# Mixture of experts: where the sorted units' way back onto the tokens stands, and which unit comes last

## The chip, the cores and the metric

The kernel runs on one core of a Trainium2 chip. The metric is the device time of one execution in microseconds (us), taken as the median of several runs. Engines are named as in the profile: PE (TensorE, matrix products), PEld (its loads of the stationary operand), DVE (VectorE), ACT (ScalarE), POOL (GpSimd) and SP (SyncE, which here only issues DMA transfers; its queue is SPq).

## The reference

One sequence of 128 tokens with 512 channels goes through three layers: attention over 12,544 context rows, self-attention with block-scaled weights, and a mixture of 32 experts. The change is in the last one, which adds this to the tokens:

```python
def _gate(x, gate_w, gate_bias):            # 4 of 32 experts for each token, weights that sum to 2
    ...
def _moe(x, topk_idx, topk_w, w1, w2, w3):  # H = 512 channels, F = 256 inside an expert
    ...
    h = silu(einsum('ech,ehf->ecf', buf, w1)) * einsum('ech,ehf->ecf', buf, w3)
    ob = einsum('ecf,efh->ech', h, w2)
    y = ob[flat_e, minimum(slot, CAP - 1)]
    ...
    return (y.reshape(n, K, H) * topk_w[:, :, None]).sum(1)
out = _moe(x, topk_idx, topk_w, w1, w2, w3)
shared = silu(x @ shared_gate) * (x @ shared_up) @ shared_down
x = x + out + shared
```

Each expert has 1.5 MB of weights in float32: w1 and w3 (512 x 256 each) and w2 (256 x 512).

## The kernel before

`fast_block` does the three layers; the mixture is its last stage, from about 950 us on. Everything is in float32, and instructions keep the order in which the program writes them (`pin`).

**Experts and units.** The first 6 experts (`FIXED`) are loaded before the gate is known. The other 26 are sorted on the chip by how many tokens chose them. Then they are worked on in *units*. A unit of kind "all" is one of the six fixed experts, over all 128 tokens. "top" is one of the two experts with most tokens, also over all 128. "wide" holds two experts with up to 64 tokens each, "narrow" four with up to 32 each; for these (`some`) the tokens of each expert were picked into columns of `picked`, and their results are put back onto the tokens by a product with `back`. The letters of L1989 give the order of the 15 units: f for all, n for narrow, t for top, w for wide.

**One unit** has these steps:

- `unit_up` (L2109): the products with w1 and w3, in four chunks of 128 channels, into one bank `up` of 512 columns. An all or top unit has one product of 128 x 512 a chunk; a wide or narrow one has two or four beside each other, in strips of 64 or 32 columns of the array ("128\*64", "128\*32" in the profile).
- `unit_act` (L2128): sigmoid on ACT, two products on DVE, into `moe_hg`. All and top units are multiplied by the gate here.
- `unit_turn` (L2141): two transpositions on PE (`hgt`), copied by ACT into `moe_ht`.
- `unit_down` (L2147): the products with w2. All and top units add them straight to `acc`, the sum over all experts that stays in one PSUM bank; wide and narrow ones write a bank `y`, which ACT copies to one of two `outs` (`moe_att_img`, `moe_qT_txt`).
- `unit_combine` (L2169), for wide and narrow units alone: a product of 128 x 512 of `back` with `outs`, added to `acc`. `back` holds the gates.

Between these stand the shared expert's parts and a test that the fast form is valid (`check_sums`, `flag`).

**The order.** In the loop from L2424, turn u takes unit u through its transposition and its way down, and unit u+1 through its way up, so that ACT and DVE work beside PE. In turn u the way back of unit u-1 stands behind the way up of u+1. The last unit's way up is written out in `last_unit` (L2174): in two halves of 256 columns, so that the sigmoid can start before the second is done, with the way back of unit u-2 in the middle.

**The loads.** Each sorted expert comes in three pieces of 512 KB: k=0 and k=1 for the two halves of its way up, k=2 for its way down. The list of all 78 pieces (L1992) follows the units, and in a unit runs over k first and over its experts then. `release` (L2200) puts a piece's buffer on the list of free ones when the program has written the product that reads it last; `load_more` (L2207) gives the next pieces in the list the next free buffers. All are issued by SP, in order; up to eight are on their way at once. A load waits until the last reader of its buffer is done.

Of the kernel before, what the change touches and what calls it, by code (L numbers as in the profile page):

```python
# [10 lines left out]
AF = mybir.ActivationFunctionType  # L11
ALU = mybir.AluOpType
# [3 lines left out]
P = 128  # L16
D = 512
NC = D // P
# [14 lines left out]
F = 256  # L33
# [737 lines left out]
def fast_block(ctx: ExitStack, tc: tile.TileContext, a: dict, out: bass.AP, amiss: bass.AP):  # L771
    nc = tc.nc
# [65 lines left out]
    def pin(ins):  # L838

        return tc.keep_in_program_order(ins)  # L840
# [46 lines left out]
    def row(tag, name, shape=(P, D)):  # L887
        return xc.tile(list(shape), FP, tag=tag, name=name)
# [7 lines left out]
    with ExitStack() as xs:  # L896
# [24 lines left out]
        m = -(-IMG // 3)  # L921
        blocks.append(("img", 0, IMG, [(o, min(m, IMG - o)) for o in range(0, IMG, m)]))
        for l0 in range(IMG, n_ctx, CHUNK):
            n = min(CHUNK, n_ctx - l0)
# [374 lines left out]
        h = rowp.tile([P, D], FP, tag="h", name="h_x")  # L1299
# [102 lines left out]
        m = heights[1]  # L1402
# [132 lines left out]
        for t in range(tile0[2], tile0[LAST]):  # L1535
            b, part, o, m = tiles[t]
# [4 lines left out]
            if t == SWITCH + 3:  # L1541
                pin(nc.tensor.matmul(
                    avp["txt"].rearrange("p g q -> p (g q)"),
                    lhsT=ident,
                    rhs=kept["av"],
                    start=False,
                    stop=False,
                    skip_group_check=True,
# [47 lines left out]
            elif t == SWITCH + 2:  # L1596
                lp = bank("l_old")
                for i in range(4):
                    r = slice(i * XHD, (i + 1) * XHD)
                    pin(nc.tensor.matmul(  # L1600
                        lp[r, :], lhsT=ones[:, :XHD], rhs=ls_old[i // 2][:, i % 2, :],
                        start=True, stop=True, skip_group_check=True,
# [42 lines left out]
        k, p = pend  # L1645
# [52 lines left out]
    def spare(name, shape=(P, 512)):  # L1698
        return ps_t.tile(list(shape), FP, tag="t", name=name)
# [170 lines left out]
    def w13_of(key, c):  # L1870
        return experts[key, c // 2][:, c % 2 * 512 : c % 2 * 512 + 512]
# [59 lines left out]
    for q in range(4):  # L1931
        for k in range(4):
# [3 lines left out]
                lhsT=aoT[:, j, :],  # L1936
                rhs=wo[q][k // 2][:, k % 2 * D : k % 2 * D + D],
                start=(j == 0),
                stop=(j == SH - 1),
# [6 lines left out]
    def halves(t):  # L1946
        return [x.rearrange("p j f -> p (j f)") for x in (t[:, :8], t[:, 8:])]
# [16 lines left out]
    picked = halves(aoT) + wo[3]  # L1964
# [21 lines left out]
    units = []  # L1986
    wide, narrow, every = some[:n_wide], some[n_wide:], [("all", [(e, 0, P)], None) for e in range(FIXED)]

    for k in "ffffnffntnwwntn":  # L1989
        units.append({"f": every, "n": narrow, "t": top, "w": wide}[k].pop(0))  # L1990
    assert not (every or narrow or top or wide)
    loads = []  # L1992
# [56 lines left out]
    def choose():  # L2049
# [43 lines left out]
    held = {  # L2093
        nm: row(tag, f"moe_{nm}", (P, 2, F))
        for nm, tag in (("sig", "part_kFalse"), ("hg", "part_vFalse"), ("ht", "part_kTrue"))
    }
# [5 lines left out]
    def add_to_acc(lhsT, rhs, last=False):  # L2102
        nonlocal n_acc
        pin(nc.tensor.matmul(acc, lhsT=lhsT, rhs=rhs, start=(n_acc == 0), stop=last))  # L2104
        n_acc += 1
# [3 lines left out]
    def unit_up(u, chunks=range(NC)):  # L2109
        kind, lanes, at_ = units[u]  # L2110
        if chunks[0] == 0:
            ups[u] = spare(f"up_{u}", (P, 2 * F))
        up = ups[u]
        for c in chunks:
            for i, r, m in lanes:
                lhsT = hT3[:, c, :] if kind != "some" else picked[c][:, at_ * P + r : at_ * P + r + m]
                pin(nc.tensor.matmul(  # L2117
                    up[r : r + m, :],
                    lhsT=lhsT,
                    rhs=w13_of((kind != "all", i), c),  # L2120
                    start=(c == 0),
                    stop=(c == NC - 1),
                    skip_group_check=True,
                ))
        if chunks[-1] == NC - 1:
            release(u, range(2))

    def unit_act(u):  # L2128
        kind, lanes, at_ = units[u]
        up = ups.pop(u)  # L2130
        sig = held["sig"][:, u % 2, :]
        hg = held["hg"][:, u % 2, :]
        pin(nc.scalar.activation(sig, up[:, :F], AF.Sigmoid))
        if kind == "some":
            pin(nc.vector.tensor_tensor(hg, up[:, :F], sig, ALU.mult))
        else:
            by = (gate if kind == "all" else gate_of)[:, lanes[0][0] : lanes[0][0] + 1]
            pin(nc.vector.scalar_tensor_tensor(hg, up[:, :F], by, sig, ALU.mult, ALU.mult))
        pin(nc.vector.tensor_tensor(hg, hg, up[:, F:], ALU.mult))

    def unit_turn(u):  # L2141
        tp = bank(f"hgt_{u}", (P, 2, P))
        for k in range(2):
            pin(nc.tensor.transpose(tp[:, k, :], held["hg"][:, u % 2, k * P : (k + 1) * P], ident))
        pin(nc.scalar.copy(held["ht"][:, u % 2, :].rearrange("p (k q) -> p k q", k=2), tp))
# [23 lines left out]
    def unit_combine(u):  # L2169
        if units[u][0] == "some":  # L2170
            k = units[u][2]
            add_to_acc(back[:, k * P : (k + 1) * P], outs[u % 2], u == len(units) - 1)

    def last_unit():  # L2174

        u = len(units) - 1
        _, lanes, at_ = units[u]
        up = [spare(f"up_{u}_{h}", (P, F)) for h in range(2)]
        for h, c in [(0, 0), (1, 0), (0, 1), (1, 1), (0, 2), (0, 3), (1, 2), (1, 3)]:
            if (h, c) == (0, 2):  # L2180
                unit_combine(u - 2)
            for i, r, m in lanes:
                pin(nc.tensor.matmul(
                    up[h][r : r + m, :],
                    lhsT=picked[c][:, at_ * P + r : at_ * P + r + m],
                    rhs=w13_of((True, i), c)[:, h * F : (h + 1) * F],
                    start=(c == 0),
                    stop=(c == NC - 1),
                    skip_group_check=True,
                ))  # L2190
            if (h, c) == (0, 3):
                sig = held["sig"][:, u % 2, :]
                pin(nc.scalar.activation(sig, up[0], AF.Sigmoid))
                hg = held["hg"][:, u % 2, :]
                pin(nc.vector.tensor_tensor(hg, up[0], sig, ALU.mult))
        pin(nc.vector.tensor_tensor(hg, hg, up[1], ALU.mult))

    index_of = {}

# [149 lines left out]
    def shared_up(nm):  # L2349
        sp[nm] = bank(nm)  # L2350
        for c in range(NC):
            pin(nc.tensor.matmul(
                sp[nm], lhsT=hT3[:, c, :], rhs=shared[nm][c], start=(c == 0), stop=(c == NC - 1)
            ))
        if nm == "shared_gate":
            pin(nc.scalar.activation(ssig, sp[nm], AF.Sigmoid))
        vec("tensor_tensor", ssig, ssig, sp[nm], ALU.mult)
        free.extend(shared_parts[nm])
        load_more()

    def shared_turn():
        t = bank("tp_shared", (P, NC, P))
        for c in range(NC):
            pin(nc.tensor.transpose(t[:, c, :], ssig[:, c * P : (c + 1) * P], ident))
        pin(nc.scalar.copy(sT, t))

    def shared_down():
        for c in range(NC):
            add_to_acc(sT[:, c, :], shared["shared_down"][c])
        free.extend(shared_parts["shared_down"])  # L2370
        load_more()

    def check_sums():

        top_over = row("top_over", "top_over", (P, 2))
        vec("tensor_reduce", top_over[:, 0:1], over, AX.X, ALU.max)
        vec("tensor_scalar", top_over[:, 0:1], top_over[:, 0:1], FAR, None, ALU.is_gt)
        vec("tensor_scalar", top_over[:, 1:2], n_within, D - 0.5, None, ALU.is_lt)
        far = row("far", "far", (P, 1))
        vec("tensor_tensor", far, top_over[:, 0:1], top_over[:, 1:2], ALU.add)  # L2380

        crowd = row("crowd", "crowd", (P, N_IN + 1))
        vec("tensor_scalar", crowd[:, :N_64], nth[:, :N_64], 64.5, None, ALU.is_gt)
        vec("tensor_scalar", crowd[:, N_64:N_IN], nth[:, N_64:], 32.5, None, ALU.is_gt)
        vec("tensor_reduce", crowd[:, N_IN:], crowd[:, :N_IN], AX.X, ALU.add)
        vec("tensor_tensor", far, far, crowd[:, N_IN:], ALU.add)
        return far

    def flag(far):
        n_far = bank("n_far")  # L2390
        pin(nc.tensor.matmul(n_far[0:1, 0:1], lhsT=far, rhs=ones[:, 0:1], start=True, stop=True))
        vec("tensor_scalar", amiss, n_far[0:1, 0:1], 1.0, None, ALU.min)
# [30 lines left out]
    n = len(units)  # L2423
    for u in range(3, n):  # L2424
        unit_turn(u)
        if u == 5:
            shared_up("shared_gate")
        elif u == 6:
            shared_up("shared_up")
            far = check_sums()  # L2430
        elif u == 7:
            shared_turn()
        elif u == 9:
            flag(far)
        elif u == 11:
            shared_down()
        if u + 1 < n - 1:
            unit_up(u + 1)
            unit_act(u + 1)
        elif u + 1 < n:  # L2440
            last_unit()
        if u != n - 2:
            unit_combine(u - 1)
        unit_down(u)

    unit_combine(n - 1)
    res = rowp.tile([P, D], FP, tag="h", name="res")
    pin(nc.vector.tensor_tensor(res, acc, x2, ALU.add))
    pin(nc.sync.dma_start(out=out, in_=res))
# [80 lines left out]
```

## Time and profile before

| | us |
|---|---|
| median of three runs | 1071.18 (1070.46 to 1071.69) |
| time of the profiled execution | 1070.2 |
| its span | 1068.5 |
| first load of a sorted expert issued | 955.55 |
| last one issued | 1048.46 |
| last product on PE starts | 1061.14 |
| last sum on DVE starts (`res`) | 1062.31 |
| output's transfer issued | 1063.03 |

The span is what the profiler recorded on the core; 1.7 us of the execution's time lie around it. Times inside are from the span's start. PE was busy 1051.4 us of the span, DVE 541.1, ACT 355.8, POOL 694.8; a busy share of PE says little here, since products in flight count as busy while the next waits. The mixture's own stretches, by the windows of the trace, have this PE time and DMA rate:

| stretch, us | PE busy | DMA, GB/s |
|---|---|---|
| 960 to 970 | 10.00 | 396 |
| 1000 to 1010 | 10.00 | 417 |
| 1040 to 1050 | 10.00 | 417 |
| 1050 to 1060 | 9.48 | 282 |
| 1060 to 1068.5 | 1.51 | 40 |

### The profile page before, as it was taken

Reading aid. Unit: us, or ns where it says so; the run is one execution under the profiler, and the core shown is the slowest. Engines: PE = TensorE matmul, PEld = TensorE weight load, DVE = VectorE, ACT = ScalarE, POOL = GpSimd, SP = SyncE. Lnnn points to the kernel's source line nnn. Section 1 sums busy time; section 2 is a strip of 40 time slices with the busy share of each in tenths; the row PEclk is TensorE's granted clock in tenths of the full one; section 3 lists DMA queues with packets and bytes.
Section 4 is the critical chain, followed back from the end, with each engine's and each line's share of the span. In section 5 each row is a group of like instructions: output and inputs, shape, how many; then the busy total and the mean of one; then the engine's idle time right before and its main releaser. Section 6 shows DMA issues by size and latency. Waiting matters only on the chain.

```text
span 1068.5 us, 24782 instructions
## 1 busy us (share of the span) xinstructions
PE 1051.4 (98%) x11076; PEld 826.6 (77%) x11076; DVE 541.1 (51%) x671; ACT 355.8 (33%) x438; POOL 694.8 (65%) x378
## 2 busy tenths in 40 slices
PE   9999999999999999999999999999999989999997
PEld 6778888888888888888888888888888769754332
DVE  3667854574445544455444554455444668432211
ACT  2353333333333333332333333333333424403111
POOL 2256888688988888888988789988899810000000
PEclk9999999999999999999999999999999999999999
DMA  8221021101111011110122301110110399619996
GB/s 318 86 81 41 2 87 44 41 1 41 40 41 40 2 40 41 40 36 7 41 84 106 99 26 41 41 40 3 39 41 2 123 361 382 229 64 410 415 413 247
DMA packets 43251, 113.24 MB, mean 106 GB/s; under 512 B 6720, under 2 KB 12032, under 8 KB 42112
## 3 DMA queue, kind: packets, MB, share of 16 engines
q1 hardware_dynamic: 43136, 111.57, 28.4%
q8 instruction: 89, 1.46, 0.5%
q14 instruction: 26, 0.21, 0.1%
HBM read 111.26 MB, written 0.29 MB: 104 GB/s over the span
## 4 chain that ended last, share of the span: by engine, by line
PE 92%; DVE 3%; POOL 2%; ACT 1%; DMA 1%; issue 0%; SPq 0%; DVEq 0%; ACTq 0%; POOLq 0%
PE kp L1082 28%; PE vp L1082 26%; PE sb L1166 9%; PE av_new L1272 8%; PE up L2117 5%; PE acc L2104 2%; PE qp L1776 1%; PE kp L1776 1%; PE yp L1934 1%; PE svp L1797 1%; PE y L2158 1%; PE vp L1234 1%; PE av_old L1272 1%; DVE p L1255 1%; DMA x<-in_x 1%; POOL sq L1127 1%
## 5 line engine op out<-in xcount | busy, mean ns | idle before, releaser
L1433 POOL TENSOR_TENSOR ls<-ls,p 128x2048 f32<-128x2048 f32 x79 | 359.7, 4553 | 21.3 <-ACT p L1263 21.3
L1263 ACT ACTIVATE p<-p 128x2048 f32<-128x2048 f32 (+1 forms) x95 | 179.9, 1894 | 444.5 <-DVE p L1255 432.9
L1255 DVE SCALAR_TENSOR_TENSOR p<-sb,rinv,mb_new 128x2048 f32<-128x2048 f32 (+1 forms) x86 | 200.0, 2326 | 129.4 <-POOL rinv L818 95.2
L1127 POOL TENSOR_TENSOR sq<-sq 128x512 f32<-128x512 f32 x96 | 96.0, 1000 | 98.2 <-ACT sq L1121 94.4
L1166 PEld LDWEIGHTS sb<-qT_txt,kraw 32*128 32x128 f32 (+1 forms) x3040 | 93.4, 186 | 32.0 <-issue 31.0
L1166 PE MATMUL sb<-qT_txt,kraw 32*128 32x128 f32 (+1 forms) x3040 | 111.5, 283 | 0.0
L1082 PE MATMUL kp<-xs,w_k_w 128*128 128x256 f32 x384 | 95.4, 391 | 0.0
L1082 PE MATMUL kp<-ctx,w_k_w 128*128 128x256 f32 x384 | 93.2, 386 | 1.0 <-ACT kp L1139 1.0
L1272 PE MATMUL av_new<-p,v 128*32 128x128 f32 (+1 forms) x2720 | 92.2, 276 | 1.0 <-ACT p L1263 1.0
L1082 PE MATMUL vp<-vt,xs 128*128 128x256 f32 x384 | 92.5, 384 | 0.0
L1082 PE MATMUL kp<-xs,kt 128*128 128x256 f32 x384 | 91.2, 380 | 0.1
L1082 PE MATMUL vp<-w_v_w,ctx 128*128 128x256 f32 x384 | 90.9, 380 | 0.0
L1082 PE MATMUL vp<-w_v_w,xs 128*128 128x256 f32 x384 | 90.8, 379 | 0.0
L1082 PEld LDWEIGHTS kp<-ctx,w_k_w 128*128 128x128 f32 x384 | 70.7, 190 | 15.0 <-issue 5.1
L1082 PEld LDWEIGHTS vp<-vt,xs 128*128 128x128 f32 x384 | 71.1, 190 | 13.3 <-ACT kraw L1110 4.5
L1082 PEld LDWEIGHTS kp<-xs,kt 128*128 128x128 f32 x384 | 72.5, 190 | 11.3 <-issue 1.1
L1082 PEld LDWEIGHTS vp<-w_v_w,xs 128*128 128x128 f32 x384 | 72.8, 190 | 10.1
L1082 PEld LDWEIGHTS vp<-w_v_w,ctx 128*128 128x128 f32 x384 | 72.8, 190 | 10.0 <-issue 0.2
L1272 PEld LDWEIGHTS av_new<-p,v 128*32 128x32 f32 (+1 forms) x2720 | 69.5, 109 | 12.3 <-ACT p L1263 2.1
L1082 PEld LDWEIGHTS kp<-xs,w_k_w 128*128 128x128 f32 x384 | 69.2, 189 | 12.6 <-issue 4.8
L818 POOL TENSOR_TENSOR rs_x<-ve_x,neghalf 128x1 f32<-128x1 f32 x3 | 1.7, 551 | 94.5 <-DVE ve_x L826 94.5
L1121 ACT ACTIVATE sq<-kraw 128x1024 f32<-128x1024 f32 x48 | 50.0, 1041 | 10.3 <-DVE kraw L1112 10.3
(460 smaller groups left out, 1442.3 us busy)
## 6 DMA issues: line engine op xcount, KB each, us to landing
ctx<-in_ctxT SPq DMA_DIRECT2D x23, 1024.0 KB, 4.9
wo<-in_experts SPq DMA_DIRECT2D x18, 512.0 KB, 9.0
wo<-in_wo_codes SPq DMA_DIRECT2D x8, 512.0 KB, 6.3
wq<-in_experts SPq DMA_DIRECT2D x8, 512.0 KB, 9.8
wk<-in_experts SPq DMA_DIRECT2D x8, 512.0 KB, 9.4
wv<-in_experts SPq DMA_DIRECT2D x7, 512.0 KB, 10.0
q<-in_experts SPq DMA_DIRECT2D x7, 512.0 KB, 10.1
f<-in_experts SPq DMA_DIRECT2D x7, 512.0 KB, 10.1
```

The source lines that it names most:

```text
L1082: pin(nc.tensor.matmul(t[:, h, :], lhsT=lhs, rhs=rhs, start=(first and h == 0 and c == 0), stop=(h == 1 and c == 1), skip_group_check=True,))
L1121: pin(nc.scalar.activation(sq[b][:, :, ks], kraw[b][:, :, ks], AF.Square))
L1127: pin(nc.gpsimd.tensor_tensor(sq[b][:, :w, ks], sq[b][:, :w, ks], sq[b][:, w : 2 * w, ks], op=ALU.add))
L1166: pin(nc.tensor.matmul(s[:m, i, g * P : (g + 1) * P], lhsT=kraw[b][rows, g, o : o + m], rhs=qT[part][rows, g, :], start=True, stop=True,))
L1234: pin(nc.tensor.matmul(vp[:m, :], lhsT=ctx_sb[0][:, c, o : o + m], rhs=vw["img"][:, c, :], start=(c == 0), stop=(c == NC - 1),))
L1255: pin(nc.vector.scalar_tensor_tensor(p[:m, k : k + n], s[:m, k : k + n], rinv[:m, t : t + 1], m_bc[part][:m, k : k + n], ALU.mult, ALU.sub ...
L1263: pin(nc.scalar.activation(p[:m, k : k + n], p[:m, k : k + n], AF.Exp))
L1272: pin(nc.tensor.matmul(avp[part][i * XHD : (i + 1) * XHD, g, :], lhsT=vv[b][:m, t - tile0[b], hd * XHD : (hd + 1) * XHD], rhs=p[:m, i, g * ...
L1433: pin(nc.gpsimd.tensor_tensor(d, d, src, op=ALU.add))
L1776: pin(nc.tensor.matmul(pp[:, k, :], lhsT=w[:, c, k * SHD : (k + 1) * SHD], rhs=hT2[:, c, :], start=(c == 0), stop=(c == NC - 1),))
L2104: pin(nc.tensor.matmul(acc, lhsT=lhsT, rhs=rhs, start=(n_acc == 0), stop=last))
L2117: pin(nc.tensor.matmul(up[r : r + m, :], lhsT=lhsT, rhs=w13_of((kind != "all", i), c), start=(c == 0), stop=(c == NC - 1), skip_group_chec ...
```

## The change

The last two units change places: the order ends with two narrow units and then the second top unit. The way back of unit u-2, no longer that of u-1, stands in turn u, and ahead of the way up of unit u+1 instead of behind it; so a unit's way up is followed at once by the way down of the unit before. In the last turn the way back of unit u-1 follows, ahead of the last way down, which goes straight to `acc`. The last unit's way up is an ordinary `unit_up`, and `last_unit` is gone.

```diff
-    for k in "ffffnffntnwwntn":
+    for k in "ffffnffntnwwnnt":
         units.append({"f": every, "n": narrow, "t": top, "w": wide}[k].pop(0))
...
-    def last_unit():
...
-        for h, c in [(0, 0), (1, 0), (0, 1), (1, 1), (0, 2), (0, 3), (1, 2), (1, 3)]:
-            if (h, c) == (0, 2):
-                unit_combine(u - 2)
...
-        if u + 1 < n - 1:
+
+        unit_combine(u - 2)
+        if u + 1 < n:
             unit_up(u + 1)
             unit_act(u + 1)
-        elif u + 1 < n:
-            last_unit()
-        if u != n - 2:
+        elif u == n - 1:
             unit_combine(u - 1)
         unit_down(u)
 
-    unit_combine(n - 1)
     res = rowp.tile([P, D], FP, tag="h", name="res")
```

More of the change, by code (lines that the diff above doesn't have):

```diff
@@ L2172, in unit_combine @@
             add_to_acc(back[:, k * P : (k + 1) * P], outs[u % 2], u == len(units) - 1)
-    def last_unit():
-        u = len(units) - 1
-        _, lanes, at_ = units[u]
-        up = [spare(f"up_{u}_{h}", (P, F)) for h in range(2)]
-        for h, c in [(0, 0), (1, 0), (0, 1), (1, 1), (0, 2), (0, 3), (1, 2), (1, 3)]:
-            if (h, c) == (0, 2):
-                unit_combine(u - 2)
[L2182 to L2196, printed above, removed]
     index_of = {}
```

## The prediction

> **What bounds the kernel now.** I read first the page's forty slices, to see what the stage of the change is made of.
>
> ```profile
> PE   9999999999999999999999999999999989999997
> DMA  8221021101111011110122301110110399619996
> GB/s 318 86 81 41 2 87 44 41 1 41 40 41 40 2 40 41 40 36 7 41 84 106 99 26 41 41 40 3 39 41 2 123 361 382 229 64 410 415 413 247
> ```
>
> A slice is 26.7 us. The last four are the mixture. There, and hardly elsewhere, the DMA engines are full (410 to 415 GB/s), while PE, too, looks busy. Which of the two sets the end is not told by shares, so next comes the chain that ended last, in order of time, over the tail (start, duration, what):
>
> ```profile
> 1037.65 3.57 PE up L2117 x32
> 1041.22 1.06 PE acc L2104 x2
> ...
> 1044.14 0.37 PE hgt L2144 x2
> 1044.51 3.44 PE up L2117 x8
> 1047.95 0.86 PE acc L2104 x2
> 1048.80 1.85 PE y L2158 x16
> ...
> 1055.81 1.91 PE acc L2104 x4
> ...
> 1058.46 1.97 PE y L2158 x16
> ...
> 1060.51 0.59 ACT moe_att_img L2166
> ...
> 1061.14 1.14 PE acc L2104 x2
> ...
> 1062.31 0.69 DVE res L2448
> ```
>
> Here PE runs from product to product and waits for no load. Then I looked at the loads of the last unit: the queue's own timeline gives the issue of each piece, and the list of DMA issues in that stretch the time from issue to landing.
>
> ```profile
> g<-in_experts SPq DMA_DIRECT2D x1, 512.0 KB, 10.0
> q<-in_experts SPq DMA_DIRECT2D x1, 512.0 KB, 10.1
> wv<-in_experts SPq DMA_DIRECT2D x1, 512.0 KB, 10.0
> ```
>
> They were issued at 1045.93, 1047.11 and 1048.46, f ahead of them at 1044.64 (10.0 as well): a piece every 1.27 us, which is 512 KB at the slices' 413 GB/s. So f lands at 1054.6, g at 1055.9, q at 1057.2, wv, the last of all 78, at 1058.5. The last unit's way down (y) starts at 1058.46, released by ACT's copy at 1058.42 and by wv at about the same moment. **PE had run behind the stream of loads and has just caught up with it at its last piece.** The end of the kernel is the landing of the last pieces plus the work that can only follow them: here 1058.46 to 1062.31, where res starts, 3.85 us. The stream itself cannot get shorter: the change loads the same 78 pieces, and the first cannot be issued before the sorting (955.55), which is not touched.
>
> **What the change moves, and its price.**
>
> *The stream.* Loads follow the order of the units, all pieces k=0 of a unit's experts, then k=1, then k=2. Up to unit 12 nothing changes. Then came three pieces of the all-token expert and twelve of the narrow unit; now twelve, then three. The narrow unit (now 13) takes the places issued from 1030.71 on, at 10.0 us from issue to landing: its first four at 1040.7 to 1044.6, its second four at 1045.8 to 1049.5, its third four at 1050.8 to 1054.6 (f). The all-token unit 14 gets g (first half of its way up) at 1055.9, q (second half) at 1057.2 and wv (way down) at 1058.5. Buffers come free in the same program order, and the last four loads reuse buffers that unit 11's way up gives back at 1031, 14 us before their issue: the stream stays as it is. Cost nothing; bounds ±0.5 us, half of the 1.2 us by which the runs before differ.
>
> *The way back onto the tokens (unit_combine) two units later.* Before it stood between two tiled runs, up and y: 1.06 us from its start to y's. Behind a full product it takes 0.86 to 0.95, behind a transposition likewise. So 0.1 to 0.2 us is saved where both neighbours were tiled: for units 9, 10 and 11, at most 0.6 us. It issues no transfer and passes none; the copy of a unit's y overwrites what the combine two units back has read by then. As many combines stand ahead of each way up as before, so no way up is later. I book it at nothing: PE then waits for the stream anyway, as the next step shows. Without that wait it would be a gain of 0.3 to 0.6.
>
> The Trainium skill, TensorEngine Tiling (Array Packing), section Tiling Modes, says that changing the tiling mode drains the engine, which speaks for putting products of one form together. The row agrees in kind (1.06 against 0.86); by the rule alone the sum would be some 0.2 us lower for each of the three places, by the row's waits it is unchanged.
>
> *Unit 13's way up* can start at about 1044.1 by PE (1044.51 less some 0.4 of the saving above), and needs its fourth piece (1044.6). Its first two chunks take half of 3.57, to 1046.4; then the third chunk's four experts wait, in order, for 1045.8, 1047.1, 1048.4 and 1049.5. From the last there are two chunks of 0.86 each: about 1051.3. Unit 12's y (1.85), unit 13's transposition (0.37) and unit 11's combine (0.86 to 1.06) follow: 1054.5. All that is queued behind the waiting products on PE; the sigmoid on ACT and two products on DVE wait with it, in time for the transposition. PE then stands for 1.4 us until g lands.
>
> *From g on, nothing is covered:* 1055.9, +0.05 to wake, +3.44 way up of unit 14 (the x8 row; its second half needs q, there by then), +1.85 y of unit 13 (x16 row), +0.37 transposition, +0.86 combine of unit 12, +0.86 combine of unit 13 (new in this place; its copy by ACT is ready 2.7 us after y's start, by the rows 1058.46 and 1060.51 + 0.59, which is 0.4 us before PE gets there), +1.91 way down of unit 14 (the x4 row). Sum 9.34, so the last product ends at 1065.3 and res starts there, against 1062.31. Unit 14's activation (sigmoid and two products on ACT and DVE; the top unit's here were done 1.4 us after its way up) lies under unit 13's y of 1.85; if that cover were gone it would cost 1.4. wv at 1058.5 is 5 us early.
>
> *The last unit's split halves* (last_unit) vanish: two of 1.86 against one of 3.57, 0.15 us of PE, and an early start of the sigmoid. Both lay ahead of the old tail and are not in the new one: nothing.
>
> **Sum:** 1065.3 − 1062.3 = +3.0 us. What stands behind res (0.69, the store, the end) is unchanged. Against its own execution: span 1068.5 becomes 1071.5, its time 1070.2 becomes 1073.2. The median of the runs shown is 1071.18, 1.0 above that execution, so 1074.2. Unknowns: waking after a landing, 0.0 to 0.3 (the one wait of a way up for a DMA in this stage, for h, is 0.3; 0.05 taken, the gap between other releases and their products here); the stream, ±0.5; the first product after idling, 0 to 0.1 (an x2 acc alone 1.14, in a run 0.86 and an end of some 0.2); the transposition, 0.27 to 0.37. Together +2.4 to +3.9, so the likeliest's own range is 1073.6 to 1075.1.
>
> **Rivals.**
>
> *Faster: the shorter ending wins.* If PE found g and q in place, only wv's products would follow the last landing: 1058.5 + 1.91 + 0.05, res at 1060.4, −1.9 us, 1069.3. For it: after the last landing there would be 1.9 us of PE in place of 3.85. Against: without waits PE would reach unit 14's way up at 1044.1 + 3.57 + 1.85 + 0.37 + 1.06 = 1050.9, so g would have to be 5 us earlier, four places ahead in the queue, and the second four pieces of unit 13 sooner too. The gain begins only when g lands 3.0 us before the time above. 0.05.
>
> *No change.* The last three pieces, with nothing behind them, land closer together, or the stream ends about 1 us sooner because earlier releases let it run without its gaps: 1072 to 1073. Against: the last three took 10.0, 10.1 and 10.0 like those before them, and the DMA share is 1.03 in each stretch from 970 to 1050. That the grouping is not in the program is not likely either: in its order the combine stands behind the transposition in each unit. 0.11.
>
> *Slower still: PE's clock.* PE stands for 1.4 us ahead of g, with pieces of 0.4 ahead of that. In the profile the granted clock fell to half 2.1 us after the last product (the mean is 0.60 between 1064 and 1066, and the last product ended at 1062.3). A wait of 1.5 us was borne without that:
>
> ```profile
> PE o_ps L1691 <- DVE attT L1690: 1.9, 3, 1.5
> 865.00:870.00 5.00, 4.35 (x12) 1.74 (x12) 3.35 (x10) 0.00 (x0) 0.00 (x0) 1.00 0.82 250
> ```
>
> (the wait ends at 865.2; the clock, third number from the end, stays 1.00). If it fell for the whole new tail, its 9.3 us would double: at most 1083. 0.05.
>
> The Trainium skill, TensorE: Matmul & The Clock Gate, section Why this matters for your kernels, asks for no gaps over about 3 us, which speaks against waiting for loads at all; by it 1.4 us costs nothing, as by the row.
>
> **How the numbers follow.** Forecast 0.79, rivals 0.05, 0.11, 0.05. What a measurement here tells from no change is about 0.2%, 2.1 us; the forecast is +3.0 (0.28%), so nearly all of its chance and the clock's is slower: 0.83; within: 0.12; faster: 0.05. The range, 1072.4 to 1075.8, takes in the likeliest's own, the upper part of the case of no change, and at both ends some of the 0.6 us by which runs stray from their median.
>
> **What would show it.** Loads as before, the last landing at 1058.5 ± 0.5. PE idling ahead of unit 13's third chunk and some 1.4 us ahead of unit 14's way up, which starts at 1056.0 with a DMA as releaser; behind it no idle PE until res at 1065.3. If PE never waits there, or if the last landing is not at 1058, the working is wrong, not only its size.

## The result, and the profile after

The changed kernel takes 1074.57 us (median of 10 runs, 1074.07 to 1075.15) against 1071.49 us (10 runs, 1070.21 to 1072.71): 3.1 us more, a ratio of 1.0027 with a 95% interval of 1.0019 to 1.0035. Forecast was 1074.2.

The slices of the page, changed kernel (busy tenths, then what the DMA engines moved; the span is 1073.2 us, a slice 26.8):

```profile
PE   9999999999999999999999999999999989999996
DMA  9221021101111011110123301110010599529995
GB/s 312 91 81 41 2 80 50 41 1 41 40 41 40 2 40 41 40 41 2 41 83 122 103 4 41 41 40 30 12 41 2 148 375 378 189 101 413 415 413 199
```

The mixture's slices show 413 to 415 GB/s, where they showed 410 to 415 before. Nothing in these rows says where the 3 us come from. The chain that ended last does, over the tail (start, duration, what):

```profile
1047.65 10.00 DMA g<-in_experts
1057.65 0.04 issue
1057.70 3.70 PE up L2117 x8
1061.40 1.85 PE y L2158 x16
1063.25 0.37 PE hgt L2144 x2
1063.62 3.45 PE acc L2104 x8
1067.07 0.02 issue
1067.10 0.69 DVE res L2423
```

In the kernel before, this stretch was PE and two copies by ACT, with no transfer in it. Now the chain goes into a transfer: g, the first piece of the last unit, lands at 1057.65, and everything from there to res follows without a gap. (Units are counted from 0, so the last two are 13 and 14.) The last three loads, g, q and wv, took 10.0, 10.1 and 10.0 us from issue to landing, the same as before; the row of the last one in the list of DMA issues:

```profile
wv<-in_experts SPq DMA_DIRECT2D x1, 512.0 KB, 10.0
```

It was issued at 1050.19 and landed at 1060.19. From there to res: 1067.10 − 1060.19 = 6.91 us, against 1062.31 − 1058.46 = 3.85 before. **The difference, 3.06 us, is as large as the loss in the times (3.1).** PE's timeline shows it standing for g (in brackets: time idle before it, and what ended that), while wv, the piece that lands last, is waited for by nobody:

```profile
1055.17 1.02 PE L2104 MATMUL acc<-moe_qT_txt,ao 128*128 128x512 f32 x2
1057.70 1.98 PE L2117 MATMUL up<-g,hT 128*128 128x512 f32 x4 [1.51 <-DMA g<-in_experts]
```

This profiled execution is 4.7 us longer than that of before, 1.6 more than the medians differ by. The rest is not the change: the first sorted load was issued 1.27 us later here (956.82 against 955.55), in layers that are the same in both, and the stream of 78 pieces took 103.4 us in place of 102.9. So the experiments are compared by their times and by two stretches of their profiles: from the last landing to res, and from the first sorted load's issue to res. The second is free of the drift ahead of the mixture, but holds the scatter of the stream (102.6 to 103.4 us in the profiles with whole loads); the first is free of that too, but means something only where PE waits for a landing or just meets it.

### The profile page after: what moved, and what is told of

It is laid out like the page before. It is cut to its first block, busy times and chain, and to the rows that moved or that the text cites. A ratio compares the mean times of both kernels' runs of the same rounds, so it can differ in the third digit from the quotient of the medians.

```text
span 1073.2 us, 24718 instructions
## 1 busy us (share of the span) xinstructions
PE 1055.0 (98%) x11044; PEld 826.4 (77%) x11044; DVE 541.2 (50%) x671; ACT 356.0 (33%) x438; POOL 695.1 (65%) x378
## 4 chain that ended last, share of the span: by engine, by line
PE 87%; DMA 5%; DVE 3%; POOL 1%; ACT 1%; issue 1%; SPq 0%; DVEq 0%; ACTq 0%; POOLq 0%
PE kp L1082 27%; PE vp L1082 26%; PE sb L1166 9%; PE av_new L1272 7%; PE up L2117 3%; DMA g<-in_experts 2%; PE qp L1776 1%; PE kp L1776 1%; PE yp L1934 1%; PE svp L1797 1%; PE acc L2104 1%; PE vp L1234 1%; DMA ao<-in_experts 1%; DMA n<-in_experts 1%; DMA wv<-in_experts 1%
## 5 line engine op out<-in xcount | busy, mean ns | idle before, releaser
L1082 PEld LDWEIGHTS vp<-w_v_w,xs 128*128 128x128 f32 x384 | 72.8, 190 | 10.1
## 6 DMA issues: line engine op xcount, KB each, us to landing
q<-in_experts SPq DMA_DIRECT2D x7, 512.0 KB, 10.1
f<-in_experts SPq DMA_DIRECT2D x7, 512.0 KB, 10.1
```

What stands on the lines that cost most here:

```text
L1082: pin(nc.tensor.matmul(t[:, h, :], lhsT=lhs, rhs=rhs, start=(first and h == 0 and c == 0), stop=(h == 1 and c == 1), skip_group_check=True,))
```

## The experiments

Each kernel ran 5 to 11 times beside runs of the kernel before on the same chip (whose medians were 1070.9 to 1071.5). "Tail" is the start of res less the last landing (issue plus time to landing, which is given to 0.1 us) in that kernel's profile; "mixture" is the start of res less the issue of the first sorted load there.

| kernel | ratio to before, 95% interval | median, us | tail, us | mixture, us |
|---|---|---|---|---|
| before | | 1071.5 | 3.85 | 106.76 |
| changed | 1.0027 (1.0019 to 1.0035) | 1074.57 | 6.91 | 110.28 |
| e_group: way back two units later alone | 0.9999 (0.9990 to 1.0008) | 1070.79 | 3.81 | 106.92 |
| e_swap: order of units alone (the split last way up goes with it) | 1.0036 (1.0022 to 1.0050) | 1074.13 | 7.56 | 110.19 |
| e_early: changed, g and q ahead of unit 13's pieces | 1.0035 (1.0021 to 1.0048) | 1075.23 | 7.72 | 111.06 |
| e_mid: changed, g and q inside unit 13's pieces | 1.0009 (1.0000 to 1.0018) | 1072.60 | 5.13 | 108.57 |
| e_tdown: before, top unit's way down last | 0.9997 (0.9988 to 1.0006) | 1071.16 | 3.54 | 106.59 |
| e_both: e_tdown and e_group | 0.9996 (0.9987 to 1.0005) | 1070.82 | 3.46 | 106.81 |
| h_before: before, half of the stream | 0.9998 (0.9989 to 1.0007) | 1071.14 | – | 106.77 |
| h_group: e_group, half of the stream | 0.9997 (0.9988 to 1.0006) | 1071.54 | – | 106.44 |
| h_after: changed, half of the stream | 0.9981 (0.9972 to 0.9990) | 1068.98 | – | 104.28 |

### Which part of the change costs: e_group and e_swap

```diff
 e_group, against before:
+        if u + 1 < n:
+            unit_combine(u - 2)
         if u + 1 < n - 1:
...
-        if u != n - 2:
+        else:
             unit_combine(u - 1)
```

> The way back two units later alone; the order of the units, the loads and the split last way up are those of before. Theory (the stream of loads sets the end): PE meets the same last landing, so the last sum (res) starts 3.85 us after the last piece's landing as before (3.6 to 4.1), and the time is that of before within 0.5 us. Rival (the regrouping itself costs, because a unit's result reaches the tokens later): most of the 3.1 us appears here.

```diff
 e_swap, against the changed kernel:
-        unit_combine(u - 2)
         if u + 1 < n:
             unit_up(u + 1)
             unit_act(u + 1)
-        elif u == n - 1:
-            unit_combine(u - 1)
+        unit_combine(u - 1)
         unit_down(u)
```

> The new order of the units alone; the way back stands behind the way up as before. Theory: the same work stands behind the landing of the last unit's first piece, in another order (3.44 + 0.86 + 1.85 + 0.37 + 0.86 + 1.91), so res starts 6.9 to 7.1 us after the last landing and the time is 3.1 us above before (2.5 to 3.6). Rival (regrouping costs): the time of before within 0.5 us.

The regrouping alone leaves time (0.9999) and tail (3.81) as they were; the new order alone has the loss (1.0036). So it is the order. In e_group PE's timeline shows where its saving ends: three experts' products of the last y start at 1058.64, when ACT's copy is there, and the fourth's half a microsecond later, when wv has landed (1059.14):

```profile
1058.64 0.62 PE L2158 MATMUL y<-f,moe_ht 128*32 128x512 f32 x1 [0.52 <-ACT moe_ht L2145]
...
1059.15 0.62 PE L2158 MATMUL y<-wv,moe_ht 128*32 128x512 f32 x1
```

The tail of e_swap, 7.56, is half a microsecond over what was expected. Its chain shows why:

```profile
1055.81 3.70 PE up L2117 x8
1059.51 0.86 PE acc L2104 x2
1060.37 1.90 PE y L2158 x16
...
1062.34 0.59 ACT moe_qT_txt L2166
1062.94 0.04 issue
1062.98 2.86 PE acc L2104 x6
```

With unit 12's combine ahead of y, nothing lies over ACT's copy of y: PE waits for it before unit 13's combine. In the changed kernel that copy is under unit 12's combine. I had added the same products in another order and forgotten that one of them was a cover. So the regrouping is worth 0.65 us here (7.56 against 6.91), in the one place where PE sets the pace; the times, with intervals of ±0.14%, don't resolve it.

### Is it the order of the loads or the order on PE: e_mid and e_early

Both are the changed kernel but for one line after the list of loads is made; every instruction on PE stands where it stood.

```diff
 e_mid:
+    loads[-7:] = loads[-3:-1] + loads[-7:-3] + loads[-1:]
 e_early:
+    loads[-15:] = loads[-3:-1] + loads[-15:-3] + loads[-1:]
```

> The changed kernel with one edit in the list of loads: the last unit's first two pieces go between unit 13's second four and third four; all instructions on PE stand as in the changed kernel. Theory: now the end of unit 13's way up is what follows a landing (its second four land as in the changed kernel, 8.9 us ahead of the last piece), and from there 1.75 + 1.85 + 0.37 + 0.95 + 3.44 + 1.85 + 0.37 + 1.72 + 1.91 run without a wait: res 5.3 us after the last landing (5.0 to 5.6), 1.5 us above before and 1.6 below the changed kernel. Rival (the loss lies in the order on PE, not in which pieces land last): no different from the changed kernel, 6.95.

> The changed kernel with one edit in the list of loads: the last unit's first two pieces go two places ahead of unit 13's twelve, its third stays last. Theory: unit 13's second four now land two places later (2.5 us), PE does its second half, unit 12's y and unit 11's combine behind that, and the last way up finds its pieces there but starts late all the same: res 8.0 us after the last landing (7.6 to 8.3), 1.0 us above the changed kernel, 4.1 above before. Rival (only the wait of 1.4 us for the last unit's first piece counts): 1.4 us below the changed kernel.

Moving two pieces of 512 KB by four places in the queue takes 1.8 us off the tail (6.91 to 5.13) and 2.0 off the time; moving them by twelve gives more than that back (7.72; expected 8.0). e_mid's rival falls: with the same order on PE the loss is a third of what it was by the times, two fifths by the tail and half by the stretch through the mixture. So does e_early's: the wait for g is gone and nothing is gained; 1.4 us below the changed kernel, a ratio of about 1.0014, lies outside its interval. That e_early is slower than the changed kernel its times don't show, as their interval holds the changed kernel's ratio; the tails do. e_mid's chain:

```profile
1040.82 9.93 DMA i<-in_experts
1050.76 0.04 issue
1050.80 1.48 PE up L2118 x9
...
1052.70 1.72 PE y L2159 x13
1054.42 0.37 PE hgt L2145 x2
1054.79 0.86 PE acc L2105 x2
1055.65 3.43 PE up L2118 x8
1059.08 1.85 PE y L2159 x16
1060.94 0.37 PE hgt L2145 x2
1061.31 3.45 PE acc L2105 x8
```

The transfer in the chain is now i, the last of unit 13's second four. g is there when PE comes to it, and no second wait follows. In e_early the chain comes from a piece of the same four (l), which lands at 1054.18, 6.3 us ahead of the last one in place of 8.9 in e_mid; 14.0 us of PE's work stand behind it in both.

### An end with the old order: e_tdown and e_both

If only a way down is to follow the last piece, the top unit need not come last, only its last piece.

```diff
 e_tdown, against before:
+    loads[-13:] = loads[-12:] + loads[-13:-12]
...
-        if u != n - 2:
+        if u < n - 2:
             unit_combine(u - 1)
-        unit_down(u)
+        if u != n - 2:
+            unit_down(u)
+    unit_down(n - 2)
```

> The kernel before, with its order of ways up (top unit, then narrow unit), but the top unit's piece for the way down loaded last of all and its way down put behind the narrow unit's, ahead of the narrow unit's way back. Theory: the narrow unit's last piece lands one place earlier (1.27 us), y runs 1.85 from there, the top unit's way down (1.7 to 1.9) covers the copy of y, the combine (0.86 + 0.2) follows: res 3.5 us after the last landing (3.2 to 3.7), 0.35 us below before, under what the times can tell. Rival (PE, not the stream, sets the old ending): no earlier than before, 3.85 or more.

> The top unit's way down last (as e_tdown) with the way back two units later (as e_group). Theory: the narrow unit's last landing sets y as in e_tdown, the 0.4 to 0.6 us that the regrouping saves on PE end in the wait for it: res 3.4 to 3.6 us after the last landing, the time 0.3 us below before, not told apart from it. Rival (savings on PE add up to the end): 3.1 or less.

The tails, 3.54 and 3.46, are the expected ones, and the times (0.9997 and 0.9996) can't tell either from the kernel before. But the tail flatters both, since wv, the last piece, has landed some 0.6 us before PE comes to it, and from the first sorted load to res they took 106.59 and 106.81 us against 106.76. So a gain is not shown, and the mechanism is in part another than the one expected. In e_tdown q, the narrow unit's last piece, landed at 1058.5, and y started at 1058.68 behind ACT's copy, which ended at 1058.64: PE and ACT set it, not the landing. PE no longer stands 0.76 us for ACT's copy of y, but it stands 0.63 us for unit 14's activation, which the top unit's way down covered before. In e_both y's products for q did wait for it, but there q took 10.8 us to land in place of 10.1, and wv 10.7; why is not known. Had q taken 10.1, it would have landed at 1057.7, before y started (1057.83). So that the regrouping's saving ends in this wait is shown for a late q alone.

### The change without the stream: h_before, h_group, h_after

```diff
+            cols = slice(k * 1024, k * 1024 + 512)
             src = a["experts"][bass.ds(index, 1), :, cols].rearrange("e p f -> (e p) f")
-        pin(nc.sync.dma_start(out=t, in_=src))
+        pin(nc.sync.dma_start(out=t if index is None else t[:, :512], in_=src))
```

> The kernel before with half of the stream: of each piece of a sorted expert only the first 512 of 1024 columns are loaded, the other half of the buffer holds what was there (so the sorted experts' results are not the reference's). Number of transfers, their order, their waits and all work on the engines are the same. Theory: the stream is done long before PE, and PE, which had only just caught up with it before, ends nearly where it did: the time of before, 0 to 1 us less. Rival (the stream had held PE back all along the mixture): several us less.

> The changed kernel with the same half of the stream. Theory: without the waits for pieces its order on PE is the shorter one: no wait for the last copy of y, a last way down that goes straight to the sum, fewer changes of form: 2.1 us below the halved kernel before (1.3 to 2.7), about 2 us below before; the change turns from a loss of 3.1 into a gain. Rival (the new order costs on PE itself): above the halved kernel before, as with whole loads.

> The way back two units later alone, with half of the stream (of each sorted expert's piece 512 of 1024 columns are loaded). Theory: without waits for loads the regrouping shows its own saving, 0.4 to 0.7 us below the halved kernel before; the rest of the halved changed kernel's 2.2 us belongs to the new last unit. Rival (regrouping is worth all of it): 2 us.

With half of the bytes the last piece lands at 1037.3 (h_before) and 1036.7 (h_after), over 20 us ahead of the end. The old order takes the same time as with whole loads (0.9998), and the same 106.8 us from the first sorted load to res: so the stream did not hold the old kernel up by anything that shows here; PE sets that end, and the last piece lands just when PE has come to it. The new order gains: 1068.98 against 1071.14 of h_before, 2.2 us less. Its chain has no transfer and no copy left in it, here from the last unit's way up on:

```profile
1051.34 3.43 PE up L2118 x8
1054.77 1.85 PE y L2159 x16
1056.63 0.37 PE hgt L2145 x2
1056.99 3.45 PE acc L2105 x8
1060.44 0.02 issue
1060.47 0.69 DVE res L2424
```

From the first sorted load's issue to res, in the three profiles: 106.77 us (h_before: 1063.30 − 956.53), 106.44 (h_group: 1063.79 − 957.35), 104.28 (h_after: 1060.47 − 956.19). So of 2.5 us the regrouping has 0.33 in the old order, a little under what I expected; the rest comes with the new last unit. How they share it in the new order stays open: there the regrouping also covers ACT's copy (0.65 in e_swap), and the new order without it was not run with half of the stream. h_group's time doesn't resolve its third of a microsecond.

## Why the prediction was right

**What bounds the kernel.** The prediction took the landing of the last pieces as what sets the old end. h_before shows that PE's own work would end there without it: half the bytes, the same time. So PE and the stream reach the last piece together. A saving on PE alone has nowhere to go then (e_group, where it ends in the wait for wv), and a change that is good for PE (h_after) loses by what it does to the order of landings.

**The stream.** Booked at nothing, ±0.5: the stream took 0.46 us more in the profile of the changed kernel, 0.2 more in e_group's (1059.14 − 956.03), and 0.28 less in e_swap's, which has the changed kernel's loads in the same order (1058.30 + 10.0 − 955.67 = 102.63). So it is scatter within that bound. The last landing stood at 1060.19, not at the 1058.5 ± 0.5 given as a sign: 1.27 us of that are the later first load, ahead of the mixture, and the rest is this scatter.

**Unit 13's way up.** Said to wait for its second four pieces and to leave PE idle for 1.4 us ahead of g; the wait was 1.51. The waits for the second four are in the trace too: weight loads waited up to 1.1 us each for n, wk and i, and PE itself stood 0.2 us for each.

**The tail.** Sum 9.34 us from g's landing; measured 1067.10 − 1057.65 = 9.45. Two terms were off and nearly cancel: the last way up took 3.70, as its first product came after idling (booked 0 to 0.1, measured 0.26; e_swap, which idles there too, has 3.70 as well, and e_mid and e_early, which don't, have 3.43), and the two combines and the way down took 3.45 as one run of eight, not 0.86 + 0.86 + 1.91 = 3.63, as in a run of eight each product takes 0.43 and the end beyond that is paid once. That the sum came out within 0.1 us owes something to luck, then; without the cancelling it would still lie in the range. Two smaller slips changed nothing: the ways up waited for a DMA three times in this stage of the kernel before, not once (weight loads for h, wv and bv, 0.3, 0.2 and 0.2 us), and a tail at half clock would have given 1083.5, not at most 1083.

**The regrouping.** Booked at nothing, as PE would wait in any case: e_group, 0.9999. Its worth without that wait was put at 0.3 to 0.6 and is 0.33. I had counted three places between tiled runs; there are two, the combines of units 9 and 10, as unit 11's stood behind a full product from the start (0.86 in the chain before, not 1.06). That it also covers a copy in the new tail, 0.65 us, I had not seen. If this saving is the drain that the Trainium skill, TensorEngine Tiling (Array Packing), section Tiling Modes, names for a change of form, it is 0.17 us a place here; no run separates the drain from the rest of such a place.

**The rivals.** "The shorter ending wins" needed g and q in place when PE comes to them; they land third and second from last, so it lost. With half of the bytes they are in place and the new order does win, by 2.2 us (h_after). That this is near the −1.9 worked out is chance: −1.9 was the last landing and one way down behind it, and in h_after the last piece lands 24 us before res, so the gain is all PE's. "No change" had the last pieces land closer together or the stream end sooner; they took 10.0, 10.1 and 10.0 us as before, and the stream was not shorter. The clock did not fall: the granted clock is 1.00 in each stretch of the tail, as the wait of 1.5 us before had let expect; what a longer wait does was not tried.

## What to carry to other kernels

Where transfers and an engine finish together, as here, look at what work stands behind each of the last pieces, not at how short the very last step is: a unit that needs its first pieces at the end of the queue puts its whole way through the engines behind them. In the old order the same unit's last piece could come last of all at no cost that shows, with its early pieces early (e_tdown). And a step that is moved may have been the cover of another engine's copy, so an equal sum of products is not an equal time.

## What was not expected of the hardware

Half of the bytes in as many transfers did not make the stream twice as fast. In h_before the 78 loads ran from 956.5 to 1037.3, 80.8 us in place of 102.9, at 239 GB/s from 960 to 1000 and 273 from 1000 to 1030, where whole pieces moved at 409 and 412. What the DMA queue waited for between 955 and 1033 us (in all, times, longest) points to the cause:

```profile
SPq L1868 <- PE up L2118: 19.9, 17, 4.6
SPq L1868 <- PE acc L2105: 3.7, 3, 2.0
SPq L1868 <- PE y L2159: 3.0, 5, 1.4
```

In the kernel before, such waits for PE's ways up were 10.5 us in 9, and most others were for an earlier transfer. With small pieces the queue waits more for PE to give a buffer back (these three rows are 26.6 of the 80.8 us), and PE's pace becomes in part the stream's. The last nine pieces landed some 0.66 us apart, about half of 1.27.
